# Reordered batch work in a convolution stage, and score matmuls of relative attention issued in another row-group order

## Chip, cores and metric

The kernel runs on one core of one Trainium2 chip. The metric is device time in microseconds, from launch to end, as the median of several runs. The profile is one further execution of the same program, recorded by the hardware profiler.

## What is computed

The reference is a perceiver of twelve residual sublayers on `x` (2 batches of 256 tokens, 256 channels) with a context of 2 x 4096 tokens, all in float32. Two of them matter here.

The first is layer 2's cross attention, which is in fact a convolution along the context, computed through Fourier transforms. It follows an int8-quantised linear layer on `x`, with which the kernel merges it:

```python
# L1_ffn (int8 linear on layernorm(x)) gives the x that enters here; ctx_1024 is z
z = z @ W_in + b_in
zn = _layernorm(z, g_ln, beta_ln)
fz = jnp.fft.rfft(zn, n=2 * L, axis=1)
...
wfh = jnp.fft.rfft(window[:, None] * h, n=2 * L, axis=0)
cwhz = jnp.fft.irfft(wfh[None] * fz, n=2 * L, axis=1)[:, :L]
dcwhz = cwhz[:, idx]
xr = _ffn(x, g1, be1, W1a, b1a, W1b, b1b)
y = xr * dcwhz
y = _ffn(y, g2, be2, W2a, b2a, W2b, b2b)
```

The second is layer 3's self attention with relative positions (16 heads of depth 16):

```python
AC = jnp.einsum('bhld,bhmd->bhlm', q + u_bias[None, :, None, :], k)
BD = jnp.einsum('bhld,hrd->bhlr', q + v_bias[None, :, None, :], r)
score = (AC + _rel_shift(BD)) / jnp.sqrt(jnp.float32(DEPTH))
attn = jax.nn.softmax(score, axis=-1)
out = jnp.einsum('bhlm,bhmd->bhld', attn, v)
```

## The kernel before

The sublayers run one after another, each as a method of one class. Inside the two stages concerned, the order of the work is written out by hand: a context manager `in_order` ties each instruction to the one before it on its engine, so that TensorE, VectorE and ScalarE (in the convolution also GpSimd, in the attention also the DMA queue of SyncE) execute in exactly the order in which the Python code emits them. An instruction that waits therefore holds up everything emitted later on its engine.

PSUM is handed out by tag, in rotation. The convolution has four banks "mm", two "tr" and two "acc"; relative attention has three "mm", three "tr" and two "acc". A rotated bank can be written again only when whoever reads its previous contents is done. A float32 matmul appears in the trace as two TensorE records.

**Convolution stage** (`int8_and_conv`, from L1437 on; its order is the list at its end, L1588 to L1634). Two chains meet in it.

- The chain of `x`: `int8_steps` is a generator of five steps (layernorm and maximum, the quantising scale, rounding, `to_T`, and last the int8 matmuls into "tr" banks with their evictions `y` by VectorE at L1410 and a GpSimd add at L1411). Two of its result tiles share a bank, and the second tile's matmul waits until the first tile has been read. Then `enter()` normalises `y` twice (moments L1545, `times` L1551) and returns `ffn2_steps`, a generator of three steps: transposes (L1421) with the evictions `yT` (L1422); the matmuls with `w1a` and the SiLU on ScalarE (`hT`, L1429, with a table load before and after); the matmuls with `w1b` and the sum (L1435).
- The chain of the context, per batch b: `project(b, u)` for u = 0 to 3 (eight matmul records, then on VectorE the sum L1499 and four small statistics L1502, L1503); `normalise(b)` (three short VectorE steps and a square root, then eight ScalarE activations L1511); `transform(b, c, part)` (eight records of 512 columns, then two VectorE products `q` at L1524, and after part 1 a subtraction and a sum on GpSimd); `back(b, c)` (sixteen records into two "acc" banks, L1535).
- `gate(b)` joins both: VectorE adds the shift to the convolved "acc" banks, multiplies with `xr`, normalises (L1579 to L1551), and a second `ffn2_steps` follows per batch.

**Relative attention** (`l3_attn`). It has eight units u (four token tiles, two halves of the heads). Each head pair occupies one of four groups of 32 rows of the array, since the contraction is over 32 rows. Three generators or functions are used per unit:

- `relative(u)`: eight matmuls of 384 columns (L2142) in row groups 0, 1, 2, 3, 0, 1, 2, 3, each into a "tr" bank, evicted to `bd` by ScalarE and VectorE in turn (L335); it yields after every second one. At its end the tile goes to DRAM and a skewed read of the unit before comes back as `bd_shift` (L2147, L2152).
- `weights(u)`: for each row group r two score matmuls of 256 columns (L2166) into one "mm" bank, then for two heads a VectorE pass that adds `bd_shift` and takes the minimum (L2170), and an exponential on ScalarE (L2174); it yields after each r.
- `turned(u)` transposes the weights (L2184, sixteen records over all 128 rows) through "tr" banks, evicted by ScalarE and VectorE in turn; `weigh(u)` multiplies with the values (L2196).

The main loop runs, for u = 0 to 9, `relative(u + 3)` and `weights(u)` alternately, step by step (`steps_in_turn`), while they exist; then `turned(u - 1)` and `weigh(u - 2)`. So for u = 0 to 4 a step is: two relative matmuls, then the scores of one row group.

Of the kernel before, what the change touches and what calls it, by code (L numbers as in the profile page):

```python
# [268 lines left out]
class Perceiver:  # L269
# [37 lines left out]
    def row(self, pool, name):  # L307

        at, n = self.row_at[name]
        t = pool.tile([P, n], F32, name=f"row_{name}")  # L310
        self.nc.sync.dma_start(t, self.dram["rows"][at : at + n].partition_broadcast(P))
        return t
# [1124 lines left out]
    def int8_and_conv(self, x):  # L1437
# [10 lines left out]
        with ExitStack() as s:  # L1448
# [20 lines left out]
            def taps(u):  # L1469
                ps = self.bank([P, 2, D])  # L1470
                for ph in range(2):
                    cols = ds(2 * P * u + ph, P, step=2)
                    self.mm(ps[:, ph, :], [(self.h1[:n, c, cols], w["l2x_wp2"][:n, c, :]) for c, n in enumerate((P, P, 65))])
                for ph in range(2):
                    at = self.win_t[:, 2 * u + ph : 2 * u + ph + 1]
                    nc.vector.scalar_tensor_tensor(filt[:, u, ph, :], ps[:, ph, :], at, row(1), ALU.mult, ALU.mult)
                    nc.scalar.activation(plain[:, u, ph, :], ps[:, ph, :], AF.Copy, scale=at)

            def tap_sums():
                ps = self.acc([P, D])  # L1480
                self.mm(ps, [(self.ones, plain[:, u, ph, :]) for u in range(2) for ph in range(2)])
                nc.vector.tensor_mul(shift, ps, row(2))

            def spectrum(c):
                ps = self.bank([P, 2, D])
                for ph in range(2):
                    self.mm(ps[:, ph, :], [(w["fh"][:, ph, u, ts(c, P)], filt[:, u, ph, :]) for u in range(2)])
                nc.scalar.copy(fs[:, c], ps)
# [5 lines left out]
            def project(b, u):  # L1494
                ps = self.bank([P, 2, D])
                for ph in range(2):
                    cols = ds(2 * P * u + ph, P, step=2)
                    self.mm(ps[:, ph, :], [(cc[b][:, k, cols], w["win"][:, k, :]) for k in range(KC)])
                nc.vector.tensor_add(zn[b][:, u], ps, row(0).unsqueeze(1).to_broadcast([P, 2, D]))  # L1499
                st = self.sm.tile([P, 2, 6], F32, name="bst", tag="bst_z", bufs=2)  # L1500
                for ph in range(2):
                    nc.vector.bn_stats(st[:, ph, :], zn[b][:, u, ph, :])  # L1502
                    nc.vector.bn_aggr(mv[b][:, 2 * u + ph, :], st[:, ph, :])  # L1503

            def normalise(b):
                r = self.rstd(mv[b][:, :, 1], 1e-5)
                less = self.sm.tile([P, 8], F32, name="less8", tag="less8")
                nc.vector.scalar_tensor_tensor(less, mv[b][:, :, 0], -1.0, r, ALU.mult, ALU.mult)
                for i in range(8):
                    at = zn[b][:, i // 2, i % 2, :]  # L1510
                    nc.scalar.activation(at, at, AF.Identity, scale=r[:, i : i + 1], bias=less[:, i : i + 1])  # L1511
# [3 lines left out]
            def transform(b, c, part):  # L1515
                ps = self.bank([P, 2, D])
                self.mm(ps, [(fz[:, u, ts(2 * part + c, P)], zn[b][:, u]) for u in range(4)])
                f_re, f_im, f_re2 = fs[:, c], fs[:, 2 + c], fs[:, 4 if c == 0 else 1]
                if part == 0:

                    got[b, c] = pool.tile([P, 4, 2, D], F32, name="q", tag=f"c{c}")
                q = got[b, c]
                for i, f in enumerate((f_re, f_im) if part == 0 else (f_im, f_re2)):
                    nc.vector.tensor_mul(q[:, 2 * part + i], ps, f)  # L1524
                if part == 1:
                    nc.gpsimd.tensor_sub(q[:, 0], q[:, 0], q[:, 2])
                    (nc.vector if (b, c) == (1, 1) else nc.gpsimd).tensor_add(q[:, 1], q[:, 1], q[:, 3])

            def back(b, c):
                for t in range(2):  # L1530
                    if c == 0:
                        convolved[b, t] = self.acc([P, D])
                    for part in range(2):
                        for ph in range(2):
                            nc.tensor.matmul(  # L1535
                                convolved[b, t], finv[:, 2 * part + c, ts(t, P)], got[b, c][:, part, ph, :],
                                start=(c, part, ph) == (0, 0, 0), stop=(c, part, ph) == (1, 1, 1),
                            )
# [18 lines left out]
            def enter():  # L1557


                xn, add = tokens("xn1"), tokens("add1", "xb8")  # L1560
                mv = moments(y8)
                var = mv[:, :, 1]
                r = self.rstd(var, 1e-5)
                both = self.sm.tile([P, NT], F32, name="both", tag="both")
                nc.vector.tensor_mul(both, var, r)
                nc.vector.tensor_mul(both, both, r)
                both = self.rstd(both, 1e-5)
                nc.vector.tensor_mul(both, both, r)
                times(xn, y8, mv, both)
                times(add, y8, mv, r)  # L1570
                for t in range(NT):
                    nc.gpsimd.tensor_add(add[:, t, :], add[:, t, :], row(3))
                return self.ffn2_steps(pool, xn, "g1", "be1", w1a, "b1a", w1b, add, xr)
# [14 lines left out]
            with self.in_order(e.PE, e.DVE, e.Activation, e.Pool):  # L1588
                xb = tokens("xb8")
                first = self.int8_steps(pool, x, xb, y8)  # L1590
                next(first)
                taps(0)
                taps(1)
                next(first)
                tap_sums()
                next(first)
                for c in range(5):
                    spectrum(c)
                next(first)
                project(0, 0)  # L1600
                project(0, 1)
                next(first, None)
                project(0, 2)
                project(0, 3)
                one = enter()
                normalise(0)
                project(1, 0)
                project(1, 1)
                next(one)
                project(1, 2)  # L1610
                project(1, 3)
                normalise(1)
                next(one)
                transform(0, 0, 0)
                next(one, None)
                transform(0, 0, 1)
                transform(0, 1, 0)
                transform(0, 1, 1)
                back(0, 0)
                transform(1, 0, 0)  # L1620
                back(0, 1)
                transform(1, 0, 1)
                two = gate(0)
                transform(1, 1, 0)
                next(two)
                back(1, 0)
                transform(1, 1, 1)
                next(two)
                back(1, 1)
                last = gate(1)  # L1630
                next(two, None)
                next(last)
                next(last)
                next(last, None)  # L1634
# [459 lines left out]
    def l3_attn(self, x):  # L2094
# [8 lines left out]
        with ExitStack() as s:  # L2103
# [50 lines left out]
            def weights(u):  # L2154


                t, half = divmod(u, 2)
                pr = shifted[u]
                nm = self.sm.tile([P, 8], F32, name="nm8", tag="nm8")
                for r in range(4):  # L2160

                    ps = self.bank([P, 2, L])
                    rows = ts(r, 32)
                    for i in range(2):
                        c = 2 * half + i
                        nc.tensor.matmul(  # L2166
                            ps[:, i, :], qu[rows, c, ts(t, P)], kT[rows, c, ts(t // 2, L)], start=True, stop=True
                        )
                    for h in (r, 4 + r):
                        nc.vector.tensor_tensor_reduce(  # L2170
                            pr[:, h, :], ps[:, h // 4, :], pr[:, h, :], -0.25, 3.0e38, ALU.add, ALU.min,
                            nm[:, h : h + 1],
                        )
                        nc.scalar.activation(pr[:, h, :], pr[:, h, :], AF.Exp, bias=nm[:, h : h + 1], scale=-1.0)  # L2174
                    yield
# [201 lines left out]
```

## Time and profile before

| quantity | value |
|---|---|
| median of 3 runs | 2697.01 us (2693.47 to 2702.94) |
| profiled execution, its own time | 2690.3 us |
| span of the profiled execution | 2688.4 us |
| TensorE busy | 2465.8 us, 92% of the span |
| VectorE busy | 1705.0 us, 63% |
| ScalarE busy | 1342.3 us, 50% |
| GpSimd busy | 918.2 us, 34% |
| granted TensorE clock, mean | 0.95 |
| convolution stage, from the first `project` record to the next layer's first transposes | 1521.21 to 1635.23 us |
| relative attention's loop, from the first scores to the last records of `weigh` | 2459.94 to 2547.61 us |

Times inside the trace are counted from the start of the span. In a timeline line the columns are: start, duration of the merged run, engine, source line, operation, output and inputs, shape, number of records, and in brackets the idle time of that engine just before, with what ended it. A line of the waits view reads: who waited, for whom, then the total in us, the number of waits, the longest. A line of the windows view has, for one stretch, the busy time and number of instructions of TensorE (matmuls, then weight loads), VectorE, ScalarE and GpSimd, then the granted TensorE clock, the busy share of the DMA engines and GB/s. Ends of matmuls are modelled by the profiler.

### The profile page before, as it was taken

The numbers are of one execution on the slowest core, as the hardware profiler recorded it, in microseconds if no ns is written. First come the engines' busy times: TensorE is split into PE (matmuls) and PEld (weight loads), VectorE is DVE, ScalarE is ACT, GpSimd is POOL, SyncE is SP. The second block draws the span as 40 slices with busy tenths as digits, with TensorE's granted clock in tenths as the row PEclk, the third lists the DMA queues.
The fourth block names the chain that finished last, engine by engine and source line by source line (L and its number), as shares of the span: only waits on it lengthen the run. The fifth ranks groups of instructions, "written<-read, shape, count | busy, mean of one in ns | idle before, by whom it ended". The sixth has DMA issues, their size and how long they took to land. (4 is left out here: it accounts for less than half of the span.)

```text
span 2688.4 us, 45255 instructions
## 1 busy us (share of the span) xinstructions
PE 2465.8 (92%) x17570; PEld 1644.2 (61%) x17571; DVE 1705.0 (63%) x3129; ACT 1342.3 (50%) x2544; POOL 918.2 (34%) x859
## 2 busy tenths in 40 slices
PE   8986999999999999999899888798799999999858
PEld 6853576666666666676434556457635665655657
DVE  5466677777777777777679636352267887844522
ACT  3323666666666666665466212341127777773411
POOL 0520265555656555556379112001101222200010
PEclk9987999999999999999899998889899999998879
DMA  6210322222242222222300100008610000005365
GB/s 253 83 56 28 116 65 70 64 71 64 70 127 65 70 64 71 64 67 78 115 2 1 63 20 24 25 33 290 224 73 18 2 2 2 2 12 188 134 228 206
DMA packets 78133, 215.53 MB, mean 80 GB/s; under 512 B 6488, under 2 KB 22176, under 8 KB 67424
## 3 DMA queue, kind: packets, MB, share of 16 engines
q1 hardware_dynamic: 72128, 202.69, 22.8%
q0 software_dynamic: 2048, 6.56, 0.7%
q10 hardware_dynamic: 3744, 3.41, 0.4%
q8 instruction: 138, 2.26, 0.3%
q14 instruction: 75, 0.61, 0.1%
HBM read 191.14 MB, written 21.50 MB: 79 GB/s over the span
## 5 line engine op out<-in xcount | busy, mean ns | idle before, releaser
L1043 POOL TENSOR_TENSOR total<-total,S 128x512 f32<-128x512 f32 x434 | 542.4, 1281 | 304.3 <-ACT S L1032 304.3
L1032 ACT ACTIVATE S<-S 128x512 f32<-128x512 f32 x512 | 301.9, 625 | 209.4 <-DVE S L1029 209.1
L1987 DVE TENSOR_REDUCE mx<-ps_mm 128x1 f32<-128x512 f32 x512 | 317.9, 684 | 74.4 <-PE ps_tr L2011 57.9
L1018 DVE TENSOR_TENSOR most<-ps_mm,most 128x512 f32<-128x512 f32 x448 | 278.2, 683 | 119.2 <-ACT S L1015 119.2
L1015 ACT COPY S<-ps_mm 128x512 f32<-128x512 f32 x512 | 262.8, 600 | 115.5 <-PE ps_mm L1008 114.7
L1029 DVE TENSOR_TENSOR S<-S,ps_dec 128x512 f32<-128x512 f32 x512 | 317.4, 678 | 0.2 <-PE ps_dec L1087 0.2
L2015 ACT ACTIVATE PT<-ps_tr 128x512 f32<-128x512 f32 x476 | 246.7, 603 | 92.3 <-PE ps_tr L2011 87.9
L358 PEld LDWEIGHTS ps_tr<-w_l1x_wv,ctxT 128*128 128x128 f32 x2048 | 247.0, 192 | 52.9 <-issue 52.6
L1055 PE MATMUL acc<-S,v 128*64 128x256 f32 x2048 | 250.8, 387 | 7.8 <-ACT v L335 5.1
L1008 PE MATMUL ps_mm<-qT,kT 64*128 64x256 f32 x2048 | 255.7, 389 | 0.0
L358 PE MATMUL ps_tr<-ctxT,w_l1x_wk 128*128 128x512 f32 x512 | 250.6, 612 | 0.4 <-PE ps_mm L358 0.4
L358 PE MATMUL ps_tr<-w_l1x_wv,ctxT 128*128 128x128 f32 x2048 | 250.2, 275 | 0.0
L1983 PE MATMUL ps_mm<-kT,qT 32*128 32x512 f32 x1024 | 248.9, 617 | 0.2 <-DVE mx L1987 0.2
L2011 PE MATMUL ps_tr<-qm,kT 32*128 32x256 f32 x1904 | 238.0, 388 | 0.0
L1008 PEld LDWEIGHTS ps_mm<-qT,kT 64*128 64x128 f32 x2048 | 187.3, 186 | 38.3 <-DVE most L1018 3.8
L1055 PEld LDWEIGHTS acc<-S,v 128*64 128x64 f32 x2048 | 136.5, 137 | 104.9 <-ACT S L1015 38.8
L2011 PEld LDWEIGHTS ps_tr<-qm,kT 32*128 32x128 f32 x1904 | 169.7, 184 | 16.7 <-issue 6.5
L2036 POOL TENSOR_TENSOR sums<-sums,part 128x256 f32<-128x256 f32 x102 | 73.7, 722 | 267.6 <-ACT part L2035 267.6
L358 PEld LDWEIGHTS ps_tr<-ctxT,w_l1x_wk 128*128 128x128 f32 x512 | 89.2, 189 | 100.9 <-issue 98.6
L2027 PE MATMUL ps_tr<-PT,v 128*32 128x256 f32 x2048 | 139.6, 385 | 0.3 <-ACT PT L2015 0.3
L335 DVE COPY v<-ps_tr 128x512 f32<-128x512 f32 x120 | 82.9, 690 | 89.2 <-PE ps_tr L358 89.1
L1983 PEld LDWEIGHTS ps_mm<-kT,qT 32*128 32x128 f32 x1024 | 85.0, 184 | 60.7 <-issue 48.4
(515 smaller groups left out, 3751.4 us busy)
## 6 DMA issues: line engine op xcount, KB each, us to landing
ctxT<-in_ctxT SPq DMA_DIRECT2D x144, 512.0 KB, 3.6
ctxT<-in_ctxT SPq DMA_DIRECT2D x16, 1024.0 KB, 6.1
w_l2f_gu<-in_l2f_gu SPq DMA_DIRECT2D x16, 1024.0 KB, 7.0
bd_dram<-bd SPq DMA_DIRECT2D x8, 1536.0 KB, 6.0
w_l3f_w<-in_l3f_w SPq DMA_DIRECT2D x11, 1028.0 KB, 7.0
w_l3f_w<-in_l3f_w SPq DMA_DIRECT2D x11, 1024.0 KB, 5.0
ctx<-in_ctx SPq DMA_DIRECT2D x8, 1024.0 KB, 4.9
w_l2f_down<-in_l2f_down SPq DMA_DIRECT2D x16, 512.0 KB, 5.0
```

The source lines that it names most:

```text
L358: self.nc.tensor.matmul(out, lhsT, rhs, start=i == 0, stop=i == len(pairs) - 1)
L1008: nc.tensor.matmul(banks[hh, i][:, j, :], k[part, ts(2 * i + j, P)], q[u][part, :], start=True, stop=True)
L1015: nc.scalar.copy(t, ps)
L1018: nc.vector.tensor_tensor(m, ps, m, ALU.max)
L1029: nc.vector.tensor_tensor(t, t, spread[u][:, hh, :].unsqueeze(1).to_broadcast([P, 2, L]), ALU.add)
L1032: nc.scalar.activation(t, t, AF.Exp)
L1043: nc.gpsimd.tensor_add(tot, tot, t)
L1055: nc.tensor.matmul(av[u][part], vs[:, 2 * i + j, part], got[hh, i][:, j, :], start=g % 8 == 0 and i + j == 0, stop=g % 8 == 7 and i + j == 2,)
L1983: nc.tensor.matmul(ps, qT[rows, 2 * half + c, ts(t, P)], kT[rows, ts(j, 512)], start=True, stop=True,)
L1987: nc.vector.tensor_reduce(mx[:, c, r, j : j + 1], ps, AX.X, ALU.max)
L2011: nc.tensor.matmul(ps[:, i, :], kT[rows, ts(2 * u + i, P)], q[rows], start=True, stop=True)
L2015: nc.scalar.activation(pt, ps, AF.Exp, scale=0.25)
```

## The change

Two orders are changed; no instruction is added or removed. In the convolution, the first batch's four projections and its normalisation are emitted ahead of the last step of the int8 layer, the second batch's projections directly after it, and the first transform before `enter()`; the two last steps of the first feed-forward are placed further back among transforms and ways back; and `back(1, 0)` is placed behind `transform(1, 1, 1)` and the second step of the second feed-forward. In relative attention, `weights` takes its row groups in the order 2, 0, 3, 1.

```diff
@@ int8_and_conv
                 next(first)
-                project(0, 0)
-                project(0, 1)
+                for u in range(4):
+                    project(0, u)
+                normalise(0)
                 next(first, None)
-                project(0, 2)
-                project(0, 3)
+                for u in range(4):
+                    project(1, u)
+                transform(0, 0, 0)
                 one = enter()
-                normalise(0)
-                project(1, 0)
-                project(1, 1)
-                next(one)
-                project(1, 2)
-                project(1, 3)
                 normalise(1)
-                next(one)
-                transform(0, 0, 0)
-                next(one, None)
                 transform(0, 0, 1)
                 transform(0, 1, 0)
+                next(one)
                 transform(0, 1, 1)
+                next(one)
                 back(0, 0)
+                next(one, None)
                 transform(1, 0, 0)
                 back(0, 1)
                 transform(1, 0, 1)
                 two = gate(0)
                 transform(1, 1, 0)
                 next(two)
-                back(1, 0)
                 transform(1, 1, 1)
                 next(two)
+                back(1, 0)
                 back(1, 1)
@@ l3_attn, weights(u)
-                for r in range(4):
+                for r in (2, 0, 3, 1):
```

## The prediction, made before the changed kernel was run

> **What bounds the kernel now.** I read the page's busy times first, then the chain of waits, then for each of the two stages the waits, the timeline of TensorE and the windows with the granted clock.
>
> ```profile
> PE 2465.8 (92%) x17570; PEld 1644.2 (61%) x17571; DVE 1705.0 (63%) x3129; ACT 1342.3 (50%) x2544; POOL 918.2 (34%) x859
> ...
> PEclk9987999999999999999899998889899999998879
> ...
> PE 23%; DVE 2%; ACT 1%; DMA 1%; issue 1%; POOL 0%; POOLq 0%; DVEq 0%; SPq 0%; ACTq 0%
> ```
>
> TensorE is the engine to serve. The chain's shares add up to under a third, so it says little more than that TensorE leads it; each stage has to be read by itself. The clock row has 8 in slices 37 and 38 of 40, where relative attention lies (a slice is 67 us), and 9 in 23 and 24, the convolution: TensorE runs part of the first, and less of the second, slower than it could.
>
> In the convolution (1521 to 1635 us) TensorE's own waits are these, from the waits view of 1520 to 1640:
>
> ```profile
> PE ps_tr L1421 <- DVE xn L1551: 6.0, 3, 3.0
> ...
> PE ps_mm L358 <- DVE yT L1422: 4.1, 2, 3.5
> ...
> PE ps_tr L418 <- DVE xn L395: 3.7, 1, 3.7
> ...
> PE ps_tr L358 <- DVE y L1410: 3.0, 2, 2.2
> ...
> PE ps_mm L358 <- ACT hT L1429: 2.6, 2, 2.4
> ```
>
> The timeline places them: y at 1525 and 1528 (2.21 and 0.75), xn at 1537.6 (3.00) for the first feed-forward and at 1598.6 (2.74 and 0.26) for gate(0), yT at 1545.8 (3.47), hT at 1558.1 (2.43), and the next layer's xn at 1631.5. Four of the five are the chain of x with nothing else ready. They cost twice, as the windows show (clock third from the right):
>
> ```profile
> 1550.00:1554.00 4.00, 4.00 (x7) 1.73 (x6) 3.48 (x12) 0.21 (x1) 0.00 (x0) 0.64 0.00 0
> ...
> 1603.00:1606.00 3.00, 3.00 (x8) 2.34 (x8) 1.13 (x3) 0.00 (x0) 0.00 (x0) 0.50 0.03 5
> ...
> 2470.00:2475.00 5.00, 5.00 (x19) 3.58 (x14) 2.53 (x11) 3.48 (x9) 0.00 (x0) 0.50 1.00 363
> ...
> 2520.00:2550.00 30.00, 22.31 (x291) 16.85 (x286) 17.50 (x64) 14.52 (x33) 0.00 (x0) 1.00 0.19 63
> ```
>
> After an idle stretch TensorE runs at half clock: finer windows put this at 1529.0-1532.7, 1549.3-1552.5 and 1600.8-1607.3, some 13 us. In relative attention it is at half at 2464.4-2481.2, 2484.9-2491.7, 2498.7-2505.3 and 2512.5-2518.5, some 36 us. But from 2520, without relative matmuls, it has gaps and keeps the full clock. The timeline of one round there (u = 3):
>
> ```profile
> 2493.03 0.91 PE L2142 MATMUL ps_tr<-rT,qv 32*128 32x384 f32 x4
> ...
> 2493.78 0.37 PE L2166 MATMUL ps_mm<-kT,qu 32*128 32x256 f32 x1
> ...
> 2496.63 0.58 PE L2142 MATMUL ps_tr<-rT,qv 32*128 32x384 f32 x1 [0.95 <-ACT bd L335]
> ...
> 2497.60 1.27 PE L2142 MATMUL ps_tr<-rT,qv 32*128 32x384 f32 x4
> ...
> 2498.67 1.91 PE L2166 MATMUL ps_mm<-kT,qu 32*128 32x256 f32 x4
> ...
> 2500.51 3.67 PE L2184 MATMUL ps_tr<-ident,bd_shift 128*128 128x128 f32 x16
> ```
>
> The first scores start 0.75 us after the two relative matmuls, which occupy row group 0 too. The last scores run alone, 1.91 us at half clock, after a relative matmul in their own row group 3. The wait of 0.95 us is for a "tr" bank: its eviction on ScalarE stands behind the exponentials of the first scores.
>
> **What the Trainium skill says.** "TensorE: Matmul & The Clock Gate", Part 1, has a clock gate of only two states, half and full, set by activity in free-running windows of 3.4 us. The trace agrees: the granted values are 0.50 and 1.00, and the changes lie at whole multiples of about 3.4 us (1600.8 to 1607.3; 2484.9, 2491.7, 2498.7, 2505.3). Here a window that is only partly idle is enough (3.0 us waited around 1598.6). The same page, Part 3, says that matmuls in different row groups run concurrently, and that a weight load overlaps only another row group's matmul. The trace agrees: in the timeline above the two relative matmuls take 0.91 us together (one record alone takes 0.48 to 0.58 us, each matmul has two), and the scores in group 0 wait. "PSUM — Partial Sum matmul accumulation buffer", PSUM bank collisions, has PSUM guarded by bank, not by address; so the second int8 tile waits for the first one's eviction (the y waits).
>
> **Part 1, the convolution: waits.** I lay the new order out with durations from the trace: project 1.81 us on TensorE and 1.82 us on VectorE; transform 3.45; way back 3.62.
> - y. The four projections of batch 0 end at 1521.2 + 7.25 = 1528.5, and the first int8 tile is done at 1528.8. But VectorE has two more projections' sums and statistics (to 1530.5) and the three short steps of normalise(0) with ScalarE's square root between (1.3 us, 1543.5 to 1544.9 before) ahead of y. So y starts at 1531.8 and TensorE goes on at 1532.2: 3.3 us, and 0.9 us for the second pair. 4.2 in place of 2.96: **+1.2**.
> - xn. TensorE does project(1, 0 to 3) and three transforms, about 17.6 us, behind y; VectorE's part of enter() (moments 2.2, chain 1.9, xn 1.4) starts after transform(0,0,0) and fits under two transforms (6.9 us). **-3.0**.
> - yT. On VectorE there stand ahead of it now add1 (2.2), normalise(1) (1.2) and four products (2.6): 7.4 us with its own evictions, against the transposes and transform(0,1,1), 1.0 + 3.45, and some lead: about 2.2 us remain of 3.47. **-1.3**.
> - hT. back(0,0), 3.6 us, now stands between w1a and w1b, and the SiLU with its table load needs about 3.7, of which most runs beside w1a: **-2.4**.
> - back(1, 0) behind transform(1,1,1): transform(1,1,1) takes the cover of yT over (3.45 for 3.62), and the SiLU gets 7.2 us of cover instead of 3.6. No wait is there now, so **0**; gate(0)'s xn wait of 3.0 stays. GpSimd's combinations of q and ScalarE's eight activations end before their readers with over 3 us to spare; the stage's DMAs are weight loads for later use and move with the buffers' release.
>
> Sum of waits: -5.5 us.
>
> **Part 1: clock.** Before: 3.5, 3.2 and 6.2 us of work at half clock, so half of it lost, 6.4 us. After: the y waits (4.2 us in 5.6) almost surely cost one window, 1.7; gate(0)'s wait costs between 0 and 3.1, by where the window falls: I take 1.7; yT's 2.2 us may or may not cost one: 0.5. Sum 3.9, so **-2.5**. Together **-8.0 us**, with ends -5 (every window falls badly) and -10.
>
> **Part 2, relative attention.** No instruction is added; what moves is who shares a row group. In the order 2, 0, 3, 1 each pair of relative matmuls is followed by scores in a group that it leaves free. In exchange each next pair finds one of its groups (2, 0, 3) taken by those scores, one score step of 0.85 us long. At full clock:
> - The first scores can start beside the first pair, 0.75 us earlier; but VectorE copies bd first, so the minimum starts some 0.35 us earlier, and so do the exponentials and the bank behind the 0.95 us wait.
> - The last scores run beside the last relative matmul: 0.85 us less on TensorE. But the last bank's eviction hangs on the exponentials on ScalarE, so of the round (12.9, 14.0 and 12.6 us for u = 2, 3, 4) about 0.5 us is gained. Three rounds: 1.5. In u = 0 and 1 the read of `bd_shift` that lands at 2469.2 (VectorE waits 0.4 us for it now) does not come earlier, since it is issued after relative(2), ahead of the loop: 0.5 for both. From u = 5 there are no relative matmuls: 0.
> - At half clock TensorE itself sets the pace, and 1.91 us of lone scores go; the row-group phase, 7.5 us in u = 3, gets shorter and denser. Of the six half-clock windows after 2481 I expect two fewer, 1.7 us each: 3.4; I take 3.0.
>
> Sum **-5.0 us**; ends: -1.5 (nothing at the clock) and -10 (most of those windows gone). The skewed reads of u = 2 on are issued two rounds before their use and land after 6.5 to 10.1 us, so a shorter round leaves them in time.
>
> **Sum.** -8.0 - 5.0 = -13.0 us, against the profiled execution's own 2690.3 us (span 2688.4): 2677.3. The median of the runs lies 6.7 us above it, so on that scale 2697.0 - 13.0 = **2684.0 us**. Later stages move rigidly, but their windows fall elsewhere: 3 us either way. A measurement of this kernel can tell 0.3%, 8.1 us, from no change.
>
> **Rivals.**
> - *The rows are bound by eviction.* For: VectorE and ScalarE each need about 6 us per round, and the 0.95 us wait is theirs. Then part 2 gives 0, and part 1 its low end, -5: 2692.
> - *The half clock goes in both stages.* Against: the gaps at y and gate(0) stay. Convolution -10, attention -12: 2675.
> - *Slower: the half clock holds.* One mechanism: in the row-group phase only a part of the array is busy, and once a window there falls under the gate's threshold at half clock, the next ones stay under it, as at 2464.4-2481.2, five windows on end. If the new order stalls (relative matmuls behind scores in groups 2, 0 and 3) enough that this lasts through u = 2 to 7, some 14 windows more are at half, 1.7 us each, 24 us, less 8 from the convolution: +14 net with 2 us from the order, 2711. It decides from 10 windows more on. Against: from 2520 on, with gaps of 0.8 to 0.9 us, the clock is full.
> - *The order does nothing.* Excluded: instructions are tied in emission order on each engine.
>
> **Chances.** Forecast 0.62 (own range 2678 to 2691; faster by over 0.3% in 0.57 of it); eviction 0.20 (0.05 faster, 0.15 the same); clock gone 0.11 (faster); clock held 0.07 (slower). Faster 0.73, the same 0.20, slower 0.07. The range leaves out the slower case and the far end of the fastest: 2672 to 2696.
>
> **What would show it.** Right: no TensorE wait on xn of enter() nor on hT of the first feed-forward; a y wait of 3 to 4 us near 1529; 7 to 9 us fewer from 1521 to the next layer's transposes; in relative attention the first L2166 record beside the first L2142 pair, the last scores no longer alone, fewer half-clock windows after 2481. Wrong: a yT wait of over 4 us, a half clock past 2520, or a loop no shorter than 87.7 us (2459.9 to 2547.6).

## The result and the profile after

The changed kernel takes 2685.44 us (median of 5 runs, 2682.41 to 2688.98), the kernel before, beside it on the same chip, 2698.23 us (2693.47 to 2702.94). The ratio is 0.9952, with a 95% interval of 0.9936 to 0.9968: 12.8 us less by the medians, where 13.0 were forecast.

The profiled execution of the changed kernel has 2685.75 us (span 2683.8), close to its median. That of the kernel before (2690.3) lies 7.9 us under its own median, so the two profiles differ by only 4.5 us. Where that comes from, in us (half clock is the time at a granted clock of 0.50):

| part of the span | before | after | half clock before | half clock after |
|---|---|---|---|---|
| up to the first `project` record | 1521.2 | 1523.7 | 71.7 | 81.9 |
| convolution, to the first matmul of layer 2's attention | 116.5 | 106.4 | 16.5 | 10.7 |
| layer 2's attention to layer 3's cross attention (unchanged code) | 777.6 | 784.7 | 89.3 | 105.4 |
| layer 3's relative attention, whole | 143.6 | 139.9 | 44.4 | 47.8 |
| the rest | 129.4 | 129.1 | 46.6 | 47.2 |

The two changed parts are 10.1 and 3.7 us shorter, and the unchanged code between them is 7.1 us longer. For that row the forecast had allowed 3 us either way. Lines below the change have moved up by three to four in the changed kernel: L2142 is L2138, L2166 is L2163, L2184 is L2181.

On the page the busy times are:

```profile
PE 2472.0 (92%) x17571; PEld 1647.5 (61%) x17571; DVE 1704.5 (64%) x3129; ACT 1343.7 (50%) x2544; POOL 919.2 (34%) x859
```

TensorE's busy time has grown by 6.2 us though it does the same work: a matmul at half clock counts longer. So this total says nothing on the change.

TensorE's waits in the convolution, 1520 to 1640 us of the changed kernel (total, number, longest):

```profile
PE ps_tr L358 <- DVE y L1410: 3.8, 2, 3.2
PE ps_tr L418 <- DVE xn L395: 3.7, 1, 3.7
PE ps_tr L1421 <- DVE xn L1551: 3.2, 2, 2.8
PE ps_mm L358 <- DVE yT L1422: 2.8, 2, 2.2
PE ps_mm L358 <- ACT hT L1429: 0.2, 1, 0.2
```

Against before: `y` 3.0 to 3.8, `xn` 6.0 to 3.2 (the wait of `enter()` is gone, that of `gate(0)` is left), `yT` 4.1 to 2.8, `hT` 2.6 to 0.2, and the next layer's `xn` unchanged. The sum is -5.7. In all, TensorE is idle for 19.4 us of the stage before and for 13.7 after. The timeline shows where:

```profile
1523.72 7.08 PE L358 MATMUL ps_mm<-w_l2x_win,c 128*128 128x256 f32 x32
...
1534.23 1.01 PE L358 MATMUL ps_tr<-w,xqT 128*128 128x256 bf16 x4 [3.21 <-DVE y L1410]
...
1536.20 9.40 PE L358 MATMUL ps_mm<-w_l2x_win,c 128*128 128x256 f32 x32
...
1562.37 7.13 PE L358 MATMUL ps_mm<-yT,w_l2x_w1a 128*128 128x512 f32 x16 [2.17 <-DVE yT L1422]
...
1596.37 0.33 PE L1421 MATMUL ps_tr<-ident,xn 128*128 128x128 f32 x1 [2.75 <-DVE xn L1551]
```

The first and the third line are the same 32 records, of batch 0 and of batch 1. The second set takes 9.40 us in place of 7.08, because it runs behind the `y` waits at half clock, as the windows show (clock third from the right):

```profile
1534.00:1541.00 7.00, 6.20 (x18) 4.64 (x18) 2.68 (x6) 3.85 (x8) 2.87 (x4) 0.51 0.00 0
1541.00:1600.00 59.00, 53.68 (x176) 32.08 (x175) 30.91 (x77) 10.18 (x18) 13.59 (x14) 1.00 0.07 23
```

From 1541 to 1600 the clock is full throughout: the waits for `yT` and `xn` cost only themselves in this execution.

One round of relative attention (u = 3) in the changed kernel:

```profile
2489.02 0.59 PE L2138 MATMUL ps_tr<-rT,qv 32*128 32x384 f32 x2
2489.03 0.69 PE L2163 MATMUL ps_mm<-kT,qu 32*128 32x256 f32 x2
...
2493.74 1.00 PE L2138 MATMUL ps_tr<-rT,qv 32*128 32x384 f32 x1 [0.30 <-ACT bd L335]
...
2494.54 0.84 PE L2138 MATMUL ps_tr<-rT,qv 32*128 32x384 f32 x1
2494.76 1.06 PE L2163 MATMUL ps_mm<-kT,qu 32*128 32x256 f32 x2
```

The first scores start 0.01 us after the first relative matmuls instead of 0.75, the last ones beside the last relative matmul, and the wait for a "tr" bank is 0.30 us instead of 0.95. The loop takes 83.9 us (2459.45 to 2543.34) in place of 87.7. But the half clock did not become rarer in this profile: after the first long stretch there are six half windows, as before, one of them past 2520 (2534.2 to 2537.6), where I had expected none.

### The profile page after: what moved, and what is told of

The parts are those of the page before. It is cut to its first block, busy times and chain, and to the rows that moved or that the text cites. A ratio compares the mean times of both kernels' runs of the same rounds, so it can differ in the third digit from the quotient of the medians.

```text
span 2683.8 us, 45256 instructions
## 1 busy us (share of the span) xinstructions
PE 2472.0 (92%) x17571; PEld 1647.5 (61%) x17571; DVE 1704.5 (64%) x3129; ACT 1343.7 (50%) x2544; POOL 919.2 (34%) x859
## 5 line engine op out<-in xcount | busy, mean ns | idle before, releaser
L335 DVE COPY v<-ps_tr 128x512 f32<-128x512 f32 x120 | 82.9, 690 | 89.1 <-PE ps_tr L358 89.0
```

## The experiments

Theory: waits and row groups act where the prediction puts them, and the clock adds a part that depends on where its windows fall. Rivals: one half of the change does it all; what is saved is lost again in later, unchanged stages. All stage lengths stand in a table after the experiments.

**Each half alone.** The changed kernel with one half taken back: `conv_only` keeps the new convolution, `rows_only` the new row order.

```diff
 conv_only, against the changed kernel
-                for r in (2, 0, 3, 1):
+                for r in range(4):
 rows_only, against the kernel before
-                for r in range(4):
+                for r in (2, 0, 3, 1):
```

> The new order of the convolution with the old row order (0, 1, 2, 3) in relative attention. Theory (two separate gains): the stage from the first projection to the next layer's transposes takes about 104 us (114.0 before, 103.9 in the changed kernel), the attention loop stays at 87 to 88 us (87.7 before), and the time falls by 8 to 10 us. Rival (the stage's gain is given back later, since unchanged stages took longer in the changed kernel's profile): the stage is 104 us, but the time falls by less than 4 us.

> The old order of the convolution with the row order (2, 0, 3, 1). Theory: the convolution stage stays at 113 to 115 us, the loop takes 82 to 85 us in place of 87.7, and the time falls by 3 to 5 us. Rival (evictions bind, the 3.8 us seen are only where the half-clock windows fell): the loop is 86 to 89 us, the time within 2 us of before.

Measured: `conv_only` 2688.75 us, ratio 0.9965 (0.9949 to 0.9981); `rows_only` 2688.66 us, ratio 0.9963 (0.9948 to 0.9977). Both halves count, some 9.4 and 10 us. Three expectations were missed: the loop of `conv_only`, with the old rows, takes 90.9 us instead of 87 to 88 (the table below comes back to this), that of `rows_only` 80.6 instead of 82 to 85, and `rows_only` gains twice what was expected. The sum of the halves, 19 us, is more than the 12.8 of both together; but each interval is 4 us wide to either side, so this difference of 6 is not resolved. In `rows_only` a round runs so, at full clock:

```profile
2498.17 0.59 PE L2142 MATMUL ps_tr<-rT,qv 32*128 32x384 f32 x2
...
2503.95 1.75 PE L2184 MATMUL ps_tr<-ident,bd_shift 128*128 128x128 f32 x12
```

From the first relative matmuls to the transposes it takes 5.8 us; the kernel before needs 7.5 (2493.03 to 2500.51), part of it at half clock. No half clock falls between 2489 and 2529 us of `rows_only`.

**Which conflict costs.** The old convolution with two other row orders. In 0, 2, 1, 3 all four scores lie in a group of the pair just issued, and none in a group of the next pair. In 3, 1, 2, 0 none conflicts with its own pair, and the next pair is met at its second matmul twice and at its first once.

```diff
-                for r in range(4):
+                for r in (0, 2, 1, 3):   (rows_0213)
+                for r in (3, 1, 2, 0):   (rows_3120)
```

> The old convolution with the row order (0, 2, 1, 3), in which the scores of every step need a row group that the relative matmuls ahead of them still occupy (before, two of the four steps do). Theory (conflicts between row groups cost the time): the loop takes longer than before, 90 to 94 us in place of 87.7, and the time rises by 2 to 6 us. Rival (evictions bind): 86 to 89 us, no change.

> The old convolution with the row order (3, 1, 2, 0): the scores of each step again use a group that the pair ahead leaves free, but the next pair's first matmul is free as well, and only its second one waits for the scores. Theory: loop 1 to 2 us shorter than with (2, 0, 3, 1), 81 to 84 us. Rival (the wait of the next pair behind the scores costs nothing, since the next bank is not free earlier): the same as (2, 0, 3, 1), within 1 us at equal clock.

Measured: `rows_0213` 2699.34 us, ratio 1.0004 (0.9993 to 1.0014), loop 89.1 us; `rows_3120` 2690.61 us, ratio 0.9963 (0.9951 to 0.9976), loop 83.9 us, the same as the changed kernel's to 0.03 us at the same place in the clock's window. For `rows_0213` the theory failed: neither the loop of 90 to 94 us nor the longer time came, and 89.1 us lies within the 87.7 to 93.0 that loops with the old order take in the table below. So no cost is seen of a conflict with the own pair in the two middle steps. What is left, by exclusion, are the conflicts of the first and the last step: the old order and 0, 2, 1, 3 have them, 2, 0, 3, 1 and 3, 1, 2, 0 do not, and only the latter two gain. Which of the two costs more was not tested. For `rows_3120` the rival was right: which matmul of the next pair stands behind the scores is of no account here.

**The `y` wait.** First seven matmuls into a bank that nobody reads fill the wait, to take the clock's share away and leave the wait. Then the wait itself is avoided, with a bank for each of the four int8 tiles. Both have the new convolution and the old rows.

```diff
 conv_fill
+            if t == 1:
+                spare = self.acc([P, D])
+                for _ in range(7):
+                    nc.tensor.matmul(spare, self.ident, xn[:, 0, :], start=True, stop=True)
 conv_y_banks
-            if t % 2 == 0:
-                ps = self.bank([P, 2, D], "tr")
-            self.mm(ps[:, t % 2, :], ...)
+            ps = self.bank([P, D], "tr" if t < 2 else "mm")
+            self.mm(ps, ...)
```

> The new convolution order, old row order, with seven more matmuls of 256 columns (about 3.1 us, into an accumulation bank that nobody reads) behind the first int8 tile, where TensorE waits 3.2 us for y. They do no needed work. Theory (the half clock that follows is caused by the idle stretch): the two half-clock windows at 1534 to 1541 go, project(1, .) runs at full clock, 7.2 us in place of 9.4, and the stage takes 100 to 102 us in place of 103.9, though work is added. Rival (the clock falls for another reason, or the added work delays y): 104 to 107 us.

> The new order of the convolution with the old row order, and each of the four int8 tiles in a PSUM bank of its own (two tr, two mm). Theory (the y waits are the shared bank's, and they alone make the two half-clock windows that follow): TensorE's waits of 3.2 and 0.6 us on y are gone, project(1, 0 to 3) takes about 7.1 us at full clock in place of 9.4, and the stage takes 98 to 101 us in place of 103.8; the time is 0 to 5 us under that of the new convolution order alone (2688.75). Rival (VectorE is behind anyway, since the statistics and normalise(0) stand ahead of y there): TensorE waits as long on a bank of project(1, .) or on VectorE's sums instead, and the stage stays at 102 to 104 us.

Measured for `conv_fill`: 2683.85 us, ratio 0.9948 (0.9928 to 0.9968), stage 102.8 us. Its timeline:

```profile
1537.78 3.19 PE L1412 MATMUL acc<-xn,ident 128*128 128x256 f32 x14
...
1542.72 7.08 PE L358 MATMUL ps_mm<-w_l2x_win,c 128*128 128x256 f32 x32
```

With 3.19 us of work that serves nothing, the next matmuls start as early and take 7.08 us instead of 9.40: without the idle time the two half-clock windows are gone. The gain on the stage is only 1.0 us, less than expected, since in this execution another window fell on `w1a` (8.83 us in place of 7.13). The median is 4.9 us under that of `conv_only`, with intervals that overlap; the profiled execution (2697.51 us) is the slowest of the six.

Measured for `conv_y_banks`: 2688.78 us, ratio 0.9967 (0.9950 to 0.9984), stage 101.7 us, close to its range of 98 to 101. The waits view of the stage has no line for `y` left; those not shown are 3.7 us for the next layer's `xn`, 1.0 ahead of the stage and 0.2 for `hT`:

```profile
...
PE ps_tr L1420 <- DVE xn L1550: 3.0, 2, 2.8
PE ps_mm L358 <- DVE yT L1421: 3.0, 2, 2.3
...
```

and the timeline has the second set of projections at full speed:

```profile
1537.46 7.24 PE L358 MATMUL ps_mm<-w_l2x_win,c 128*128 128x256 f32 x32
```

So TensorE waits because of the shared bank; that VectorE is late sets only how long (the next experiment shortens it), and does not hold the projections. That PSUM is to be guarded by bank and not by address is the rule that the Trainium skill gives ("PSUM — Partial Sum Buffer", PSUM bank collisions; the prediction has the title otherwise), and the trace agrees: 3.8 us of waits vanish with the sharing.

One rival is left for the half clock behind the wait: the stages of `conv_fill` and `conv_y_banks` begin 1.30 and 1.05 us after a point of the clock's grid (explained with the table below), that of the changed kernel 3.29. Two kernels further below both begin at 3.34. `conv_gate_cover` has the `y` wait and `best` has not; here are the same 32 records of the two:

```profile
1536.34 9.38 PE L358 MATMUL ps_mm<-w_l2x_win,c 128*128 128x256 f32 x32
```
```profile
1530.24 7.24 PE L358 MATMUL ps_mm<-w_l2x_win,c 128*128 128x256 f32 x32
```

So at an equal place, too, the half clock goes with the idle time. The median of `conv_y_banks` does not show the gain: its interval is 4.6 us to either side, it equals that of `conv_only` (2688.75), and in the profile one window fell behind `yT` and two behind `gate(0)`.

**Normalisation behind `y`.** `normalise(0)` after the last int8 step instead of ahead of it, to let VectorE reach `y` sooner.

```diff
                 for u in range(4):
                     project(0, u)
-                normalise(0)
                 next(first, None)
+                normalise(0)
```

> The new convolution order, old row order, but with normalise(0) behind the last step of the int8 layer instead of ahead of it. Theory: y starts on VectorE without the three short steps of normalise(0), so that the first y wait of 3.2 us becomes about 2, and with it one half-clock window may go: stage 101 to 103.5 us in place of 103.9. Rival: ScalarE's eight activations then end later and transform(0,0,0) waits for them: stage 104 to 106 us.

Measured: 2690.0 us, ratio 0.9969 (0.9957 to 0.9980); the `y` waits fall to 3.1 us, by 0.7, but the stage takes 106.2 us, 2.3 more than with the new order at the same place in the window (13.9 us at half clock in place of 8.2). A shorter wait, and a longer stage. The length is the rival's, but not its cause: no wait of TensorE for ScalarE's activations is there. Half clock fell on `w1a` (8.83 us in place of 7.13) and behind `gate(0)`, where the new order has none at this place.

**The wait of `gate(0)`.** `transform(1, 1, 1)` ahead of the second feed-forward's first step.

```diff
                 two = gate(0)
                 transform(1, 1, 0)
+                transform(1, 1, 1)
                 next(two)
-                transform(1, 1, 1)
+                back(1, 0)
                 next(two)
-                back(1, 0)
                 back(1, 1)
```

> The new convolution order, old row order, with transform(1,1,1) ahead of the first step of the second feed-forward, and back(1,0) between its first and second step. Theory: gate(0)'s xn wait (2.75 and 0.40 us) goes, since 6.9 us of transforms cover VectorE's chain, and the evictions yT are covered by the way back: stage 100 to 102 us in place of 103.9. Rival: VectorE then has transform(1,1,1)'s products and sum (2.5 us) ahead of yT, and a yT wait of 1 to 3 us takes the place: 103 to 104 us.

Measured: 2687.12 us, ratio 0.9965 (0.9955 to 0.9976), stage 100.8 us, 3.0 less than the new order at the same place in the window. The median is 1.6 us under that of `conv_only`, with intervals that overlap. The transposes follow on the last transform without a wait, and a way back covers `yT`:

```profile
1597.01 0.76 PE L1421 MATMUL ps_tr<-ident,xn 128*128 128x128 f32 x4
1597.61 3.62 PE L1535 MATMUL acc<-q,finv 128*128 128x256 f32 x16
```

**`back(1, 0)`.** The new convolution with `back(1, 0)` at its old place.

```diff
                 next(two)
+                back(1, 0)
                 transform(1, 1, 1)
                 next(two)
-                back(1, 0)
                 back(1, 1)
```

> The new order of the convolution with the old row order, but with back(1, 0) at its old place ahead of transform(1, 1, 1). Theory (the prediction's: this move is worth 0): stage 103 to 105 us, as with the new order (103.8), the wait of gate(0) unchanged at 2.8 us. Rival (the way back is the better cover at its new place): TensorE waits 1 to 3 us more on hT of the second feed-forward or on the bank of its sum, and the stage takes 105 to 107 us.

Measured: 2692.33 us, ratio 0.9982 (0.9972 to 0.9993), stage 107.0 us. That is the rival's length without the rival's cause; the waits are those of the new order:

```profile
PE ps_tr L358 <- DVE y L1410: 4.0, 2, 3.2
...
PE ps_tr L1421 <- DVE xn L1551: 3.0, 2, 2.7
PE ps_mm L358 <- DVE yT L1422: 2.8, 2, 2.2
```

The longer stage is half clock, 13.9 us of it. The next kernel has `back(1, 0)` at its new place and happens to begin the stage at the same place in the window: it takes 109.1 less its own delay of 2.2, 106.9. So the move is worth 0 in the stage. The median is 3.6 us above that of `conv_only`, with intervals that overlap.

**A delay.** The changed kernel with three multiplications by 1.0 at the end of the stage, which change nothing but the time at which the next layer begins.

```diff
                 next(two, None)
+                for _ in range(3):
+                    nc.vector.tensor_scalar_mul(out[:, 2:4, :], out[:, 2:4, :], 1.0)
```

> The changed kernel, with three multiplications by 1.0 of 512 elements in place on VectorE at the end of the convolution stage, on the path to the next layer: 1 to 2 us of delay there and nothing else. Theory (how long the unchanged stages take depends on where in the stage the clock's windows of 3.4 us fall): the sublayers from layer 2's attention to layer 3's cross attention do not take 784 to 785 us as in the three kernels with the new order and no delay, but something else, as 777 to 782 us, and the time moves by something other than the delay, by -5 to +4 us. Rival (later stages move rigidly): they take 784 to 785 us again, and the time is 1 to 2 us longer than the changed kernel's.

Measured: 2685.27 us (2682.93 to 2690.69), ratio 0.9956 (0.9944 to 0.9968). VectorE's timeline shows the delay, and TensorE waits 5.9 us for the next layer's `xn` in place of 3.7:

```profile
1629.08 2.31 DVE L1632 TENSOR_SCALAR xres<-xres 128x512 f32<-128x512 f32 x3
```

A delay of 2.2 us on the path moves the median by -0.2; with some 3 us of spread to either side, that is not enough to tell it from 2.2. The later stages together take 783.9 us, near the rival's 784, so the theory's 777 to 782 failed. But they are not rigid: layer 2's attention takes 83.4 us in place of 86.0, and the first part of the feed-forward behind it, up to its router, 82.4 in place of 79.9.

**All together.** A bank for each int8 tile, `transform(1, 1, 1)` ahead, `back(1, 0)` between, and the new row order (`best`; its edits are those above).

> The whole change, with each int8 tile in a bank of its own, and with transform(1, 1, 1) ahead of the second feed-forward's first step and back(1, 0) between its steps. Theory (the stages' gains add where they arise): convolution stage 95 to 98 us in place of 103.9, relative attention's loop 81 to 84 us, time 2676 to 2682 us. Rival (what is gained in the convolution is given back by half-clock windows in the unchanged stages that follow): the convolution is as short, but the sublayers from layer 2's attention to layer 3's cross attention take 785 us or more in place of 777.6, and the time is 2683 us or more.

Measured: 2672.89 us (5 runs, 2668.82 to 2677.16), ratio 0.9914 (0.9897 to 0.9931). It beats both kernels, the changed one by 12.6 us by the medians and by 10 by the ratios. The convolution takes 94.2 us (1522.5 to 1616.7), and no half clock falls in it; the whole stage in one window:

```profile
1522.45:1616.66 94.21, 87.20 (x330) 59.70 (x329) 53.46 (x137) 23.51 (x42) 23.76 (x35) 1.00 0.08 26
```

The convolution is a little shorter than expected, the loop (83.3 us) as expected, and the unchanged stages take 782.4 us, 4.8 more than before: some is given back, less than the rival had it. The time lies below the theory's range.

**The table.** In each of the thirteen profiles all changes of the granted clock lie on a grid of 3.4133 us. "At" is how long after the last grid point a stage's first matmul starts (the convolution, layer 2's attention, layer 3's relative attention as a whole). "Later" is the unchanged code from layer 2's attention to layer 3's cross attention. All in us.

| kernel | conv. order | rows | at | conv. stage | at | later | at | loop | half clock in loop |
|---|---|---|---|---|---|---|---|---|---|
| before | old | 0123 | 2.42 | 114.0 | 2.88 | 777.6 | 2.24 | 87.7 | 37.5 |
| rows_only | old | 2031 | 1.29 | 115.1 | 2.84 | 777.6 | 2.23 | 80.6 | 29.9 |
| rows_0213 | old | 0213 | 1.27 | 115.1 | 2.83 | 777.7 | 2.24 | 89.1 | 43.4 |
| rows_3120 | old | 3120 | 2.53 | 117.2 | 2.72 | 782.4 | 0.09 | 83.9 | 40.6 |
| after | new | 2031 | 3.29 | 103.9 | 0.43 | 784.7 | 0.07 | 83.9 | 40.6 |
| conv_only | new | 0123 | 3.31 | 103.8 | 0.42 | 784.6 | 3.36 | 90.9 | 51.0 |
| conv_fill | new, filled | 0123 | 1.30 | 102.8 | 0.58 | 784.4 | 3.36 | 90.9 | 51.1 |
| conv_y_first | variant | 0123 | 3.30 | 106.2 | 2.72 | 780.6 | 1.66 | 93.0 | 57.6 |
| conv_gate_cover | variant | 0123 | 3.34 | 100.8 | 0.60 | 782.7 | 1.66 | 90.9 | 51.0 |
| conv_y_banks | new, banks | 0123 | 1.05 | 101.7 | 2.81 | 777.6 | 2.19 | 92.7 | 57.2 |
| conv_back_old | variant | 0123 | 2.43 | 107.0 | 2.71 | 782.3 | 3.39 | 90.9 | 51.0 |
| after_delay | new, delay | 2031 | 2.46 | 109.1 | 1.15 | 783.9 | 3.40 | 84.0 | 40.8 |
| best | all edits | 2031 | 3.34 | 94.2 | 0.81 | 782.4 | 1.56 | 83.3 | 37.5 |

Rows with different places in the window mix the code with the place. Rows with nearly the same place are fairer to compare, but the place does not fix a length either: with the same old rows the loop takes 87.7 us at 2.24 (`before`) and 92.7 at 2.19 (`conv_y_banks`), and 93.0 and 90.9 both at 1.66.

The loops can be compared without the place. With the rows 2, 0, 3, 1 they take 80.6 to 84.0 us (four profiles), with 0, 1, 2, 3 they take 87.7 (`before`) and 90.9 to 93.0 (six others). Most of the difference is half clock at the beginning of the loop. With the old rows six of the seven profiles have 10 or 11 windows on end at half clock there; with 2, 0, 3, 1 and with 3, 1, 2, 0 all five have 6. Here is that stretch of `conv_only`, then of `after_delay`:

```profile
2459.71:2493.84 34.13, 33.10 (x124) 24.18 (x124) 17.42 (x64) 18.24 (x41) 0.00 (x0) 0.50 0.74 260
```
```profile
2464.62:2485.10 20.48, 20.16 (x82) 14.75 (x84) 11.25 (x43) 12.73 (x28) 0.00 (x0) 0.50 0.89 315
```

The profile of the kernel before, with 5 such windows, is the exception among the seven, and the prediction was made from it.

The column "later" goes with the place, whatever the code before it, to within one half-clock window (1.7 us of time): 777.6 or 777.7 for the four kernels at 2.81 to 2.88, one of them with the new convolution; 784.4 to 784.7 for three at 0.42 to 0.58, but 782.7 at 0.60; 782.4, 782.3 and 780.6 at 2.71 and 2.72. The windows of that part, of the kernel before, then of `conv_y_banks`, then of the changed kernel:

```profile
1637.73:2415.33 777.60, 704.34 (x7043) 452.38 (x7043) 464.69 (x870) 391.99 (x800) 111.30 (x155) 0.94 0.17 59
```
```profile
1633.84:2411.46 777.62, 704.62 (x7043) 452.67 (x7043) 464.62 (x870) 391.89 (x800) 111.54 (x155) 0.94 0.17 59
```
```profile
1630.08:2414.79 784.71, 711.86 (x7043) 456.58 (x7043) 464.74 (x870) 392.21 (x800) 111.55 (x155) 0.93 0.17 58
```

All three have the same 7043 matmul records, and VectorE is busy for the same 464.6 to 464.7 us. Only TensorE's busy time grows, by 7.5 us, with the clock at 0.93 in place of 0.94.

## Why the prediction was right, point by point

- **Waits of the convolution, -5.5:** -5.7 in the waits views. `y` +0.8 (forecast +1.2), `xn` -2.8 (-3.0), `yT` -1.3 (-1.3), `hT` -2.4 (-2.4). The wait that grew, `y`, has the cause that was given (the shared bank, `conv_y_banks`). This term does not depend on the place: TensorE is idle for 19.4 or 19.5 us of the stage in all four profiles with the old order, and for 13.6 or 13.7 in the changed kernel, `conv_only` and `conv_back_old`.
- **`back(1, 0)`, 0:** right (`conv_back_old`: the same waits, the same stage at the same place in the window).
- **Clock of the convolution, -2.5:** right on the scale of the profiles, where half clock falls from 14.0 to 8.2 us; TensorE works for 12.7 and 6.1 us of it, which is worth 3.3. But which wait costs a window was not as forecast: `y` cost two, `gate(0)` none and `yT` none. In `conv_back_old`, at 2.43, it was one, two and one, 13.9 us, as many as before. So this term lies between 0 and some -3, by the place in the window. The stage went from 114.0 to 103.9 us, -10.1, the far end of the forecast's -5 to -10 and more than the "7 to 9 us fewer" of its signs; at the same place in the window (2.42 against 2.43) it is -7.0. Waits and clock leave some 1.1 us of both figures over, by which TensorE's busy time is shorter even at full clock; it was not forecast, and its cause is open.
- **Order of the rows at full clock, -2.0, and its clock, -3.0:** both right in kind and too small in size, and the clock's gain lies partly elsewhere than forecast. In the changed kernel's own profile the loop is 3.8 us shorter with as many half-clock windows after 2481 as before, and one past 2520. Taken alone, that would speak against the clock's term, and past 2520 it is what I had named as a sign of error. Other pairs show more. `conv_only` against `after_delay` (3.36 and 3.40): -6.9, of which 10.2 us less half clock is worth 5.1, 3.0 windows, and the order itself 1.8. Before against `rows_only` (2.24 and 2.23): -7.1, 7.6 us less half clock worth 3.8, 2.2 windows, and the order 3.3; this pair rests on the exceptional profile. "Two fewer of six" after the first long stretch does not hold as it was put: in the first pair the long stretch itself falls from 10 windows to 6, with 5 and 6 windows after it; in the second it goes from 5 to 6, and the windows after it fall from 6 to 3. That from 2520 on the clock stays full was one execution's case.
- **The next pair behind the scores, put at no cost:** not contradicted, and not shown. `rows_3120` shows only that it does not matter which matmul of the next pair is met; no run has the new order without any.
- **"Later stages move rigidly, 3 us either way":** wrong. In the profiles they gave 7.1 us back. Over several executions this may average out in part (no run shows it), since each begins somewhere else on the grid: the first matmul of the program lies at 0.09 to 3.09 us in the thirteen profiles.
- **The sum:** forecast -13.0; measured -12.8 between the medians (interval of the ratio: -8.6 to -17.3). The closeness to 0.2 us is luck: alone, the halves measure some -9.4 and -10 against -8.0 and -5.0, and the later stages move by up to 7 us between profiles.

Of the rivals, "bound by eviction" falls: the wait for a "tr" bank went from 0.95 to 0.30 us in the round shown, and `rows_only` gains by itself. "The half clock holds" did not come for the new order; it is rather the old one that holds it, for 10 or 11 windows in six of its seven profiles. "The half clock goes in both stages" came in part in the attention. What stays open is whether the two halves add (9.4 and 10 against 12.8), and whether the spread of one kernel's runs, 10 us and more, comes from the place in the window. The profiles suggest it: the unchanged code ahead of the first `project` takes 1521.0 to 1530.6 us in the thirteen, with 71.7 to 88.7 us of half clock. But the place of an execution that was not profiled isn't known.

## What to carry to other kernels

On an engine-bound kernel, count a stage's waits from the trace: here that sum came within 0.2 us. Count the clock's share as a range, and compare two kernels' stages over several profiles of each: one profile can be an exception, as that of the kernel before was, and even two that begin at the same place in the clock's window can differ by some us. A gain in one stage of a few us can come back as a loss of the same size in unchanged code, so take the verdict from the median of several runs and not from two profiles. A PSUM bank that two short results share can hold TensorE for microseconds: here it was 3.8 us of wait and two windows behind it, and a bank for each tile, together with a cover for the other wait, brought another 10 to 12.6 us, close to what the whole change had brought.

## What was not expected of the hardware

- The unchanged part of 780 us has a length that goes with where it begins on the grid: 782.3 us at 2.71 and 777.6 at 2.81, a tenth of a microsecond apart. The Trainium skill ("TensorE: Matmul & The Clock Gate", Part 1) states a free-running window of 3413 ns, in which a kernel's start falls somewhere else in each run; the grid of 3.4133 us agrees, and so does the program's first matmul, at 0.09 to 3.09 us after a grid point. It puts the cost of warming up under 1% of a typical span. The 7.1 us seen here are under 1% as well, but as large as the changes under study.
- The busy time in a window, as the profile counts it, does not tell whether the clock drops. These are windows of the changed kernel, laid on the grid, the first in the loop and the others at its end:

```profile
2489.82:2493.23 3.41, 3.41 (x22) 2.06 (x18) 2.50 (x11) 2.56 (x6) 0.00 (x0) 1.00 0.87 271
2523.95:2527.36 3.41, 2.47 (x20) 1.80 (x15) 2.85 (x17) 2.56 (x7) 0.00 (x0) 1.00 0.00 0
2530.78:2534.19 3.41, 2.47 (x20) 1.68 (x15) 2.70 (x15) 2.23 (x6) 0.00 (x0) 1.00 0.02 5
```

TensorE is busy for 2.47 us in both of the last two; the clock stays full after the first of them and drops to half after the second. It also drops after the window of the first line, in which TensorE is busy throughout, all of it with matmuls of 32 rows. And from 2459 to 2479 it is busy for 19.79 of 20 us, mostly with matmuls of 32 rows, at 0.50. What the gate counts these runs don't settle.
